# Softmax statistics of a quantised cross-attention: row maxima taken from logits in PSUM, row sums by a product with ones

## The chip, the cores and the metric

The kernel runs on one core of a Trainium2 chip. The core has five engines that each work through their own queue in order: TensorE (PE in the profile, with its weight loads shown apart as PEld), VectorE (DVE), ScalarE (ACT), GpSimd (POOL) and SyncE (SP), which here issues the transfers between HBM and SBUF. TensorE writes to PSUM, which is divided into eight banks of 128 partitions by 512 fp32 numbers[...]. Engines wait for each other by semaphores. The metric is the time of one execution on the device in microseconds (us), the median over several executions.

## The reference

Four transformer blocks follow one another, each with its own weights, on hidden states `x` of shape 4 x 1024 x 288 (batch, tokens, width), with a context of 4 x 64 x 288 that all of them attend to. Blocks 0 and 3 are attention, cross-attention and feed-forward with quantised linear layers; block 1 is a cross-attention; block 2, the one that matters here, quantises the operands of its attention. What is computed in its second attention, the cross-attention to the context, is this, with 16 heads of width 18 and 8 bits throughout:

```python
def _fake_quant(x, n_bits, always_zero=False):
    levels = float(2 ** n_bits - 1)
    if always_zero:
        delta = max(x) / levels; zp = 0.0
    else:
        delta = (max(x) - min(x)) / levels; zp = round(-min(x) / delta)
    xq = clip(round(x / delta) + zp, 0.0, levels)
    return (xq - zp) * delta

def _quant_attention(x, ctx, Wq, Wk, Wv, Wo, bo):
    q = x @ Wq; k = ctx @ Wk; v = ctx @ Wv           # split in 16 heads
    q, k, v = fake_quant of each
    probs = softmax(q . k / sqrt(18))                # 4 x 16 x 1024 x 64
    probs = _fake_quant(probs, 8, always_zero=True)
    return (probs @ v) @ Wo + bo

n2 = _ln(h, ln2_g, ln2_b)
h = h + _quant_attention(n2, encoder_hidden_states, Wq2, Wk2, Wv2, Wo2, bo2)
n3 = _ln(h, ln3_g, ln3_b)
a, gate = split(n3 @ Wff1 + bff1)
h = h + a * gelu(gate) @ Wff2 + bff2
```

The point to keep in mind is the step of the last quantisation, `delta`. It needs the largest probability over all batches, tokens, heads and context tokens, so no probability can be rounded before every one has been seen.

## The kernel before, in words

The 4096 tokens are handled as 32 tiles of 128 (`NT`, eight for each batch, `NTB`). Each head's 18 columns are padded to 32 (`HP`), so that four heads make a head group of 128 rows and there are four groups (`NG`). The blocks run one after the other, with some work of the next block placed in the current one: during block 2 the weights of block 3 are loaded (line L1568), and their quantisation scales are formed on DVE (lines L1581 to L1612, tiles called `ssw` and `wps`).

The function that the change touches is `fq_tail`. It does the context attention and the feed-forward of block 2. The queries before quantisation, `rawq`, lie in DRAM, with their global maximum and minimum known. Keys and values have been quantised and laid out as block-diagonal operands: `kbd4` holds, for each batch and head group, a 128 x 256 matrix whose four diagonal blocks are the keys of four heads, and `kbd` holds the same keys in the other orientation, in blocks of 64 rows for two heads. Because of `delta`, the attention makes two passes over the logits.

The *first pass* finds, for each token and head, the largest exponential (`top`, 128 x 32 x 16) and the sum of the exponentials (`sums`, of the same shape). Its loop takes the tiles one by one. For a tile t it does the following.

- DVE scales, shifts and rounds the queries in two operations (`fq_levels`, L818 and L819), and clips them in a third (L3302), which writes them as bf16 in the padded layout into one of three buffers, `pads`.
- TensorE transposes the four head groups (L3308) into a PSUM bank, ACT copies them to SBUF (L3312, `qT`), and SP stores them to DRAM (L3313, `qb`) for the second pass.
- TensorE makes the logits, tokens on partitions, in four bf16 products of 128 x 256 (L3318), two to a bank. ACT takes the exponential of each bank, 128 x 512 (L3325), into an SBUF tile `e` of 128 x 16 x 64 fp32. The softmax scale and the quantisation steps come in as the scale of this activation.
- DVE reduces `e` to its 16 maxima (L3331). GpSimd adds the two halves of every head's 64 exponentials (L3333, 512 outputs for each partition) and again the halves of these (L3335, 256 outputs), and DVE sums the 16 values that remain for each head (L3336).

No exponential of the first pass is shifted by a maximum. The PSUM pool of this stage, `psum8`, has eight buffers of one bank; the SBUF pool of work tiles, `f2k0`, has three buffers for each kind of tile. The order in which the instructions of different tiles stand in each engine's queue is not that of the source: it is decided when the program is built, by the scheduler of the framework. An engine then follows its queue strictly.

After the loop `prob_shift` forms, on DVE, the reciprocals of `sums` (L2483), the product with `top`, the largest probability (across partitions with GpSimd), and a logarithmic shift for each token and head, split into three bf16 numbers (`parts`). The *second pass* (`probs`) begins with loads of `qT` from DRAM (L3362), adds the shift to spare rows of the queries, recomputes the exponentials in the transposed layout (context tokens on partitions), rounds them and multiplies them with the values. It is woven with the feed-forward (`forward`) of earlier tiles, and with block 3's weights. Ahead of it SP loads the feed-forward's weights (`w1` and `w2`, L2517, L114, L3352).

Two helpers return PSUM buffers: `ps1` a bank (from pool `pb`) and `ps2` two neighbouring banks (from pool `pa`). The pool set `psum_attn` exists already for other stages: three buffers of two banks and two of one bank.

Of the kernel before, what the change touches and what calls it, by code (L numbers as in the profile page):

```python
# [28 lines left out]
F32 = mybir.dt.float32  # L29
BF16 = mybir.dt.bfloat16  # L30
I32 = mybir.dt.int32
AF = mybir.ActivationFunctionType
ALU = mybir.AluOpType
AX = mybir.AxisListType
PSUM = bass.MemoryType.PSUM

P = 128
B, S, C, H, D, T, FF = 4, 1024, 288, 16, 18, 64, 1152
NTB = S // P
NT = B * NTB  # L40
CK, NC3 = 96, 3
HP = 32
NG = 4
# [1136 lines left out]
class Fast(Net):  # L1180
# [2080 lines left out]
    def fq_tail(self, w, kq, keep, rawq, mx, nmn, beside):  # L3261
# [4 lines left out]
        tc, nc = self.tc, self.nc  # L3266
        with ExitStack() as es:
# [4 lines left out]
            kt = {k: gp.tile(keep[k][1], BF16, name=k) for k in ("kbd", "vbd")}  # L3272
            qb = [dr.tile([P, NG, S], BF16, name=f"qb{b}") for b in range(B)]
            with (
                self.psum8("f2"),
                tc.tile_pool(name="f2q", bufs=1) as qp,
                self.work("f2k0", 3),
            ):
                kt["kbd4"] = qp.tile(keep["kbd4"][1], BF16, name="kbd4")
                for k, (d, _) in keep.items():  # L3280
                    nc.sync.dma_start(kt[k], d)
                top = qp.tile([P, NT, H], F32, name="top")
                sums = qp.tile([P, NT, H], F32, name="sums")
                qn = qp.tile([P, NT, C], F32, name="qn")
                for b in range(B):
                    nc.sync.dma_start(qn[:, b * NTB : (b + 1) * NTB, :], rawq[b])
                pads = [qp.tile([P, H, HP], BF16, name=f"pads{n}") for n in range(3)]
                for pd in pads:
                    nc.gpsimd.memset(pd, 0.0)
                q = self.global_params(gp, mx, nmn, "qq")  # L3290
                self.watch_range(-0.5, 255.5, q["zp"], "qzext")
                step = gp.tile([P, 1], F32, name="step")
                nc.vector.tensor_scalar(
                    step, q["d"], kq["d"][:, 0:1], SCALE, ALU.mult, ALU.mult
                )
                rstep = self.scale_register("cstep", step)

                for t in range(NT):
                    b, j = divmod(t, NTB)
                    pd = pads[t % 3]  # L3300
                    self.fq_levels(qn[:, t, :], q, 0)
                    nc.vector.tensor_scalar(  # L3302
                        pd[:, :, :D], self.heads(qn[:, t, :]), q["top"], None, ALU.min
                    )
                    ps = self.ps1(BF16)
                    pf = pd.rearrange("p h d -> p (h d)")
                    for g in range(NG):
                        nc.tensor.transpose(  # L3308
                            ps[:, g * P : (g + 1) * P], pf[:, g * P : (g + 1) * P], self.idb
                        )  # L3310
                    qT = self.wk.tile([P, NG, P], BF16, tag="qT1", name="qT1")
                    nc.scalar.copy(qT, ps[:, : NG * P].rearrange("p (g t) -> p g t", t=P))  # L3312
                    nc.sync.dma_start(qb[b][:, :, j * P : (j + 1) * P], qT)  # L3313
                    e = self.wk.tile([P, H, T], F32, tag="e1", name="e1")
                    for m in range(2):
                        ps = self.ps1()
                        for g in (2 * m, 2 * m + 1):
                            nc.tensor.matmul(  # L3318
                                ps[:, (g % 2) * 256 : (g % 2 + 1) * 256],
                                lhsT=qT[:, g, :],  # L3320
                                rhs=kt["kbd4"][:, b, g, :],
                                start=True,
                                stop=True,
                            )
                        nc.scalar.activation(  # L3325
                            e[:, 8 * m : 8 * m + 8, :],
                            ps.rearrange("p (h k) -> p h k", k=T),
                            AF.Exp,
                            scale=rstep,
                        )  # L3330
                    nc.vector.tensor_reduce(top[:, t, :], e, AX.X, ALU.max)  # L3331
                    e2 = self.wk.tile([P, H, T // 2], F32, tag="e2", name="e2")
                    nc.gpsimd.tensor_tensor(e2, e[:, :, : T // 2], e[:, :, T // 2 :], ALU.add)  # L3333
                    e4 = self.wk.tile([P, H, T // 4], F32, tag="e4", name="e4")
                    nc.gpsimd.tensor_tensor(e4, e2[:, :, : T // 4], e2[:, :, T // 4 :], ALU.add)  # L3335
                    nc.vector.tensor_reduce(sums[:, t, :], e4, AX.X, ALU.add)  # L3336
                pd, parts = self.prob_shift(gp, qp, top, sums, step)
            pv = gp.tile([P, 1], F32, name="pv")
            nc.vector.tensor_tensor(pv, pd, kq["d"][:, 1:2], ALU.mult)
# [304 lines left out]
```

## Time and profile before

| What | Value |
|---|---|
| Time, median of 3 executions | 4930.05 us (4927.19 to 4931.08) |
| Profiled execution, its own time | 4923.53 us |
| Its span on the core | 4921.8 us, 63638 instructions |
| Mean granted TensorE clock | 0.852 |
| Busy: PE | 4244.9 us (86%), 23227 instructions |
| Busy: PEld | 1704.0 us (35%) |
| Busy: DVE | 3001.9 us (61%), 6707 instructions |
| Busy: ACT | 3066.1 us (62%), 4347 instructions |
| Busy: POOL | 1259.5 us (26%), 1900 instructions |

The span runs from the first to the last recorded instruction; the time of the execution holds a little more around it. In the views, a line such as L3331 is a line of the kernel's source, and `out<-in` names the tiles that an instruction writes and reads with their shape (partitions x elements). A group's line gives the number of its instructions, their busy time and the mean of one, and after that the time that the engine stood idle just before them with what ended most of that wait. In the view of the slices the span is cut into 40 equal parts; each digit is the busy share of one part in tenths, and the row PEclk gives the TensorE clock that was granted, in tenths of full speed. Busy time is an average over stages that have different limits, so that the shares in the table say little of any one stage; the stretch of the changed loop has to be read by itself.

### The profile page before, as it was taken

What the parts mean: (1) busy time and instruction counts of PE and PEld (TensorE: products, weight loads), DVE (VectorE), ACT (ScalarE), POOL (GpSimd) and SP (SyncE); (2) the same over time, 40 slices, a digit from 0 to 9 for tenths busy, and PEclk for the clock granted to TensorE, in tenths of its full rate; (3) what the DMA queues carried; (4) which work ended last, traced back from release to release, by engine and by line L of the source; (5) the groups of instructions that cost most, each with busy time, mean ns of one, the idle gap of its engine ahead of it and who ended that gap; (6) DMA issues with size and microseconds to landing.
All of it is one profiled execution on the core that took longest, in us unless ns stands there. A gap on an engine that the chain in (4) does not pass through costs nothing. (4 is left out here: it accounts for less than half of the span.)

```text
span 4921.8 us, 63638 instructions
## 1 busy us (share of the span) xinstructions
PE 4244.9 (86%) x23227; PEld 1704.0 (35%) x23227; DVE 3001.9 (61%) x6707; ACT 3066.1 (62%) x4347; POOL 1259.5 (26%) x1900
## 2 busy tenths in 40 slices
PE   4999998778998979998888873899998999998776
PEld 2223223445565411110233331455443223222343
DVE  8355445764654589999788878333235355445775
ACT  2776775665663279998888853212113776775796
POOL 2001001543222576410112224111111001003664
PEclk9999999889999955555688885899998999998888
DMA  3000002100001221000010022101000000001000
GB/s 84 3 5 21 10 10 75 41 31 7 11 15 52 114 63 33 26 7 0 22 28 24 23 93 69 32 10 34 1 3 17 2 4 29 7 12 38 12 17 21
DMA packets 137700, 135.98 MB, mean 28 GB/s; under 512 B 69276, under 2 KB 114972, under 8 KB 135712
## 3 DMA queue, kind: packets, MB, share of 16 engines
q1 hardware_dynamic: 136176, 128.13, 8.7%
q0 software_dynamic: 1200, 3.69, 0.3%
q8 instruction: 184, 3.01, 0.3%
q14 instruction: 140, 1.15, 0.1%
HBM read 79.92 MB, written 43.47 MB: 25 GB/s over the span
## 5 line engine op out<-in xcount | busy, mean ns | idle before, releaser
L2082 ACT ACTIVATE e<-ps 128x1024 f32<-128x1024 f32 x1024 | 992.6, 1021 | 412.5 <-PE ps L2072 405.2
L2072 PE MATMUL ps<-qT,kT 32*128 32x512 f32 x4096 | 625.9, 649 | 1.6 <-DVE sext L1994 1.6
L3110 DVE TENSOR_REDUCE top<-e 128x2 f32<-128x2048 f32 x256 | 563.5, 2274 | 13.9 <-ACT e L3103 13.8
L2028 PE MATMUL ps<-e,v 128*32 128x512 f32 x4096 | 556.8, 615 | 8.5 <-DVE oT L2039 8.5
L3479 PE MATMUL ps<-qk 32*128 32x512 bf16 x1024 | 499.7, 605 | 40.6 <-ACT e L3103 38.7
L3528 ACT ACTIVATE e<-ps 128x1024 f32<-128x1024 f32 x512 | 484.0, 1054 | 77.5 <-PE ps L3519 58.8
L3103 ACT ACTIVATE e<-ps 128x1024 f32<-128x1024 f32 x512 | 520.1, 1151 | 6.9 <-PE ps L3479 3.7
L1807 POOL TENSOR_TENSOR x<-x,y 128x288 f32<-128x288 f32 x192 | 153.3, 807 | 789.3 <-DVE y L1806 483.8
L3531 DVE TENSOR_SCALAR eb<-e 128x2048 bf16<-128x2048 f32 x256 | 321.8, 1261 | 47.2 <-ACT e L3528 45.0
L3519 PE MATMUL ps<-qk,kz 64*128 64x512 bf16 x1024 | 228.6, 444 | 43.5 <-ACT e L3528 40.3
L2546 PE MATMUL psf<-hT,w 128*128 128x512 f32 x576 | 257.9, 600 | 0.6 <-ACT hT L2538 0.6
L2072 PEld LDWEIGHTS ps<-qT,kT 32*128 32x128 f32 x4096 | 184.5, 185 | 201.9 <-issue 128.7
L1427 POOL TENSOR_TENSOR h<-h,g 128x288 f32<-128x288 f32 x160 | 130.7, 818 | 427.4 <-ACT h L1424 417.9
L2028 PEld LDWEIGHTS ps<-e,v 128*32 128x32 f32 x4096 | 81.7, 109 | 403.9 <-issue 345.2
L3479 PEld LDWEIGHTS <-qk 32*128 32x128 bf16 x1024 | 53.2, 100 | 464.7 <-issue 463.7
L3428 ACT ACTIVATE gl<-psf,bf 128x512 f32<-128x512 f32 x72 | 46.0, 684 | 269.2 <-PE psf L2550 264.7
L1924 POOL TENSOR_TENSOR v<-y,wv1b 128x288 f32<-128x288 f32 x64 | 51.7, 812 | 563.3 <-DVE y L1921 563.3
L1356 ACT COPY qT<-ps 128x640 bf16<-128x640 bf16 (+3 forms) x252 | 149.4, 640 | 74.4 <-PE ps L1351 74.2
L1351 PE MATMUL ps<-idb,q 128*128 128x128 bf16 (+2 forms) x1128 | 108.2, 241 | 89.8 <-ACT q L1335 58.9
L3432 DVE SCALAR_TENSOR_TENSOR u<-psf,bf,gl 128x512 f32<-128x512 f32 x72 | 51.1, 746 | 218.5 <-ACT gl L3428 218.5
L278 PEld LDWEIGHTS <-qT 98*128 98x128 bf16 (+2 forms) x1344 | 133.8, 104 | 119.6 <-issue 47.0
L2039 DVE COPY oT<-ps 128x512 f32<-128x512 f32 x64 | 44.1, 690 | 211.3 <-PE ps L2028 211.3
(509 smaller groups left out, 7877.2 us busy)
## 6 DMA issues: line engine op xcount, KB each, us to landing
raw<-y SPq DMA_DIRECT2D x32, 432.0 KB
in<-raw SPq DMA_DIRECT2D x30, 432.0 KB
kz<-qk SPq DMA_DIRECT2D x128, 64.0 KB
wn<-in_L_wfc SPq DMA_DIRECT2D x12, 432.0 KB
x<-in_x SPq DMA_DIRECT2D x4, 1152.0 KB
vvo<-vt SPq DMA_DIRECT2D x16, 288.0 KB
vo<-vvo SPq DMA_DIRECT2D x4, 1152.0 KB
rawq<-y SPq DMA_DIRECT2D x32, 144.0 KB
```

Source lines behind the costliest of these rows:

```text
L1356: nc.scalar.copy(qT[:, c0 : c0 + r, j0 * P : (j0 + per) * P].rearrange("p c (a t) -> p a c t", a=per), ps[:width, : per * r * P].rearrange ...
L1807: nc.gpsimd.tensor_tensor(self.x[:, t, :], self.x[:, t, :], y, ALU.add)
L2028: nc.tensor.matmul(acc[i * HP : (i + 1) * HP, :], lhsT=st["v"][:, kt, h * (D + 1) : h * (D + 1) + HP], rhs=es_[i // 2][:, i % 2, :], start ...
L2072: nc.tensor.matmul(pss[i // 2][:, i % 2, :], lhsT=self.row_tile(kT, i)[:, kt * P : (kt + 1) * P], rhs=self.row_tile(qT, i)[:, qh * 512 : ( ...
L2082: nc.scalar.activation(e, ps, AF.Exp, scale=SCALE)
L2546: nc.tensor.matmul(o, lhsT=lhs(i)[:, c, :], rhs=rhs(i)[:, c, :], start=(c == 0), stop=False)
L3103: nc.scalar.activation(e[:, j, :].rearrange("p (a n) -> p a n", a=2), sc, AF.Exp, scale=rstep, accum_out=sums[:, t, h0 + j : h0 + j + 1],)
L3110: nc.vector.tensor_reduce(top[:, t, h0 : h0 + 2], e, AX.X, ALU.max)
L3479: self.last = self.nc.tensor.matmul(ps[:, c, :], lhsT=self.row_tile(qT, i)[:, g, qt * P : (qt + 1) * P], rhs=self.row_tile(kT, i)[:, g, c ...
L3519: nc.tensor.matmul(pss[i][:, n, :], lhsT=kz[rows, i, kt * P : (kt + 1) * P], rhs=qT[rows, g, qh * 512 : (qh + 1) * 512], start=True, stop= ...
L3528: nc.scalar.activation(e[:, 2 * n : 2 * n + 2, :], ps, AF.Exp, scale=step)
L3531: nc.vector.tensor_scalar(eb, e, MAGIC, MAGIC, ALU.add, ALU.subtract)
```

## The change

The first pass of block 2's context attention is rewritten. The stage's PSUM becomes `psum_attn`. Two constants are made by GpSimd ahead of the loop: `pick`, 128 x 2 x 32 in fp32, whose column k is one on the 64 rows that belong to head k of a group, and `back`, 128 x 16, a selection of columns of the identity.

`largest(t, qT)` is the part for one tile. Quantisation, transposes, copy and store are as before, but the copy goes to a quarter of a `qT` tile that holds four tiles' tokens. The four products of logits go to one buffer of two banks, and DVE reduces the logits to their maxima straight from PSUM. The exponential is applied to the finished `top` once, at the end of the loop.

`total(n, qT)` is the part for the sums of four tiles, 512 tokens. For each head group TensorE makes the logits a second time, with context tokens on the partitions (two products of 64 x 512), ACT takes their exponential (128 x 1024, fp32), and two fp32 products with `pick` add the exponentials over the partitions, into 32 partitions of an accumulator bank `acc` for each group. ACT copies the accumulator to SBUF (`sT`), four small fp32 products with `back` turn it so that tokens lie on partitions, and DVE copies the 128 x 64 result into `sums`. `total` is a generator with a pause after each exponential and after the copy; the loop advances it by one step after each tile of the next four. GpSimd's two additions and DVE's sum are gone.

```diff
@@ -3272,7 +3272,7 @@
             kt = {k: gp.tile(keep[k][1], BF16, name=k) for k in ("kbd", "vbd")}
             qb = [dr.tile([P, NG, S], BF16, name=f"qb{b}") for b in range(B)]
             with (
-                self.psum8("f2"),
+                self.psum_attn("f2"),
                 tc.tile_pool(name="f2q", bufs=1) as qp,
                 self.work("f2k0", 3),
             ):
@@ -3295,7 +3295,19 @@
                 )
                 rstep = self.scale_register("cstep", step)
 
-                for t in range(NT):
+                pick = qp.tile([P, 2, HP], F32, name="pick")
+                nc.gpsimd.memset(pick, 0.0)
+                for k in range(4):
+                    rows = slice(k % 2 * 64, (k % 2 + 1) * 64)
+                    nc.gpsimd.memset(pick[rows, k // 2, k : k + 1], 1.0)
+                back = qp.tile([P, H], F32, name="back")
+                nc.gpsimd.tensor_copy(
+                    back.rearrange("p (g i) -> p g i", i=4),
+                    self.idf.rearrange("p (g k) -> p g k", k=HP)[:, :, :4],
+                )
+
+                def largest(t, qT):
+
                     b, j = divmod(t, NTB)
                     pd = pads[t % 3]
                     self.fq_levels(qn[:, t, :], q, 0)
@@ -3308,32 +3320,64 @@
                         nc.tensor.transpose(
                             ps[:, g * P : (g + 1) * P], pf[:, g * P : (g + 1) * P], self.idb
                         )
-                    qT = self.wk.tile([P, NG, P], BF16, tag="qT1", name="qT1")
                     nc.scalar.copy(qT, ps[:, : NG * P].rearrange("p (g t) -> p g t", t=P))
                     nc.sync.dma_start(qb[b][:, :, j * P : (j + 1) * P], qT)
-                    e = self.wk.tile([P, H, T], F32, tag="e1", name="e1")
-                    for m in range(2):
-                        ps = self.ps1()
-                        for g in (2 * m, 2 * m + 1):
+                    ps = self.ps2()
+                    for g in range(NG):
+                        nc.tensor.matmul(
+                            ps[:, g // 2, g % 2 * 256 : (g % 2 + 1) * 256],
+                            lhsT=qT[:, g, :],
+                            rhs=kt["kbd4"][:, b, g, :],
+                            start=True,
+                            stop=True,
+                        )
+                    nc.vector.tensor_reduce(
+                        top[:, t, :], ps.rearrange("p a (h k) -> p (a h) k", k=T), AX.X, ALU.max
+                    )
+
+                def total(n, qT):
+
+                    acc = self.ps1()
+                    for g in range(NG):
+                        ps = self.ps2()
+                        for pr in range(2):
+                            rows = slice(pr * 64, (pr + 1) * 64)
                             nc.tensor.matmul(
-                                ps[:, (g % 2) * 256 : (g % 2 + 1) * 256],
-                                lhsT=qT[:, g, :],
-                                rhs=kt["kbd4"][:, b, g, :],
-                                start=True,
-                                stop=True,
+                                ps[:, pr, :], lhsT=kt["kbd"][rows, n // 2, g, :],
+                                rhs=qT[rows, g, :], start=True, stop=True,
                             )
-                        nc.scalar.activation(
-                            e[:, 8 * m : 8 * m + 8, :],
-                            ps.rearrange("p (h k) -> p h k", k=T),
-                            AF.Exp,
-                            scale=rstep,
+                        e = self.wk.tile([P, 2, 512], F32, tag="e1", name="e1")
+                        nc.scalar.activation(e, ps, AF.Exp, scale=rstep)
+                        yield
+                        for pr in range(2):
+                            nc.tensor.matmul(
+                                acc[g * HP : (g + 1) * HP, :], lhsT=pick[:, pr, :],
+                                rhs=e[:, pr, :], start=(pr == 0), stop=(pr == 1),
+                            )
+                    sT = self.wk.tile([P, 512], F32, tag="sT", name="sT")
+                    nc.scalar.copy(sT, acc)
+                    yield
+                    ps = self.ps1()
+                    for j in range(4):
+                        nc.tensor.matmul(
+                            ps[:, j * H : (j + 1) * H], lhsT=sT[:, j * P : (j + 1) * P],
+                            rhs=back, start=True, stop=True,
                         )
-                    nc.vector.tensor_reduce(top[:, t, :], e, AX.X, ALU.max)
-                    e2 = self.wk.tile([P, H, T // 2], F32, tag="e2", name="e2")
-                    nc.gpsimd.tensor_tensor(e2, e[:, :, : T // 2], e[:, :, T // 2 :], ALU.add)
-                    e4 = self.wk.tile([P, H, T // 4], F32, tag="e4", name="e4")
-                    nc.gpsimd.tensor_tensor(e4, e2[:, :, : T // 4], e2[:, :, T // 4 :], ALU.add)
-                    nc.vector.tensor_reduce(sums[:, t, :], e4, AX.X, ALU.add)
+                    nc.vector.tensor_copy(
+                        sums[:, 4 * n : 4 * n + 4, :].rearrange("p t h -> p (t h)"),
+                        ps[:, : 4 * H],
+                    )
+
+                running = []
+                for n in range(NT // 4):
+                    qT = self.wk.tile([P, NG, 512], BF16, tag="qT1", name="qT1")
+                    for j in range(4):
+                        largest(4 * n + j, qT[:, :, j * P : (j + 1) * P])
+                        running = [t for t in running if next(t, running) is not running]
+                    running.append(total(n, qT))
+                while running:
+                    running = [t for t in running if next(t, running) is not running]
+                nc.scalar.activation(top, top, AF.Exp, scale=rstep)
                 pd, parts = self.prob_shift(gp, qp, top, sums, step)
             pv = gp.tile([P, 1], F32, name="pv")
             nc.vector.tensor_tensor(pv, pd, kq["d"][:, 1:2], ALU.mult)
```

## The prediction

> **What bounds the kernel now.** I read the page's slices first, to find the stage, and the granted TensorE clock beside it.
>
> ```profile
> PE   4999998778998979998888873899998999998776
> DVE  8355445764654589999788878333235355445775
> PEclk9999999889999955555688885899998999998888
> ```
>
> A slice is 123 us. The changed loop lies in slice 24 (2952 to 3075), the only one in the middle where PE falls to 3, and the clock there is 5, half. Stretches of the trace around it (columns: PE, PEld, DVE, ACT, POOL busy, clock, DMA share, GB/s):
>
> ```profile
> core 0: us, PE busy (x) PEld busy (x) DVE busy (x) ACT busy (x) POOL busy (x), PEclk, DMA share, GB/s
> 1750.00:2300.00 550.00, 506.00 (x1216) 73.02 (x1217) 536.11 (x253) 524.68 (x1012) 239.87 (x265) 0.50 0.08 23
> 2940.00:3044.00 104.00, 49.65 (x256) 27.51 (x256) 93.86 (x168) 53.03 (x97) 64.27 (x64) 0.50 0.26 66
> 3128.00:3188.00 60.00, 60.00 (x204) 32.73 (x203) 16.74 (x55) 6.89 (x11) 4.54 (x6) 1.00 0.01 1
> ```
>
> The loop takes 104 us; DVE is busy in 93.9 of them, TensorE in 49.7. Note the row above it: PE busy in 92% of the time does not bring the full clock. The groups of the stage (out<-in, count | busy us, mean ns | idle before, releaser):
>
> ```profile
> L3333 POOL TENSOR_TENSOR e<-e 128x512 f32<-128x512 f32 x32 | 40.5, 1265 | 38.9 <-ACT e L3325 38.5
> L3331 DVE TENSOR_REDUCE top<-e 128x16 f32<-128x1024 f32 x32 | 38.6, 1208 | 3.1 <-ACT e L3325 3.0
> ...
> L3308 PE MATMUL ps<-idb,pads 128*128 128x128 bf16 x128 | 19.9, 311 | 33.3 <-DVE pads L3302 33.3
> L819 DVE TENSOR_SCALAR qn<-qn,qqnzp 128x288 f32<-128x288 f32 x32 | 19.1, 598 | 0.0
> ...
> L818 DVE TENSOR_SCALAR qn<-qn,qqrd 128x288 f32<-128x288 f32 x32 | 15.5, 494 | 0.0
> L3302 DVE TENSOR_SCALAR pads<-qn,qqtop 128x288 bf16<-128x288 f32 x32 | 14.2, 443 | 0.0
> ...
> L3336 DVE TENSOR_REDUCE sums<-e 128x16 f32<-128x256 f32 x32 | 13.0, 407 | 7.1 <-POOL e L3335 7.1
> ```
>
> So DVE bounds the loop: TensorE's largest wait, 33.3 us, is for DVE's padded queries. The loop's last sum (L3336) ends at 3044.06, and the chain to the second pass starts there:
>
> ```profile
> 3043.64 0.42 DVE L3336 TENSOR_REDUCE sums<-e 128x16 f32<-128x256 f32 x1 [0.36 <-POOL e L3335]
> 3043.98 0.16 DVE L1584 TENSOR_SCALAR ssw<-ssw 128x4 f32<-128x4 f32 x1
> 3044.05 0.15 DVE L1583 TENSOR_TENSOR ssw<-wps 128x4 f32<-128x4 f32 x1
> 3044.12 3.35 DVE L2483 RECIPROCAL rs<-sums 128x512 f32<-128x512 f32 x1
> ```
>
> Every microsecond by which the last sum moves, the end moves.
>
> [...] L819 has a median of 362 ns but a mean of 598 and a longest of 1312. [...] The trace agrees on the window (its clock changes at multiples of 3.41 us). To find the measure I weighted each product's streaming time by its share of array rows times columns, window by window over the whole trace: a window at half clock is followed by full clock from a share of 0.72 up (7 of 378 windows contradict), a full one is followed by half below 0.37 (9 of 915). Busy time alone separates worse (23 contradict). [...] the trace shows some 0.15 us (eight 128*32 products of 0.43 us of streaming hold TensorE for 0.58 at 3118.16).
>
> **The change part by part.** *Removed:* GpSimd's halvings (40.5 + 24.0 us), DVE's 32 sum reductions (0.33 us from start to start, 10.5), and the blocking: L818, L819 and L3302 cost 48.8 us where 32 x 3 x 0.28 = 27 would do. DVE would need 0.84 + 1.2 = about 2.05 us a tile (the maximum now comes from PSUM[...]) and a 64-element copy per four tiles: some 66 us, plus about 14 of block 3's weights (some 6 of them now in the stage, the rest behind it). The 64 exponentials of 128x512 become 32 of 128x1024 (such rows cost 1.02 to 1.05). All this buys nothing unless DVE still bounds.
>
> *Added on TensorE:* 64 bf16 products of 64x512 (in pairs on two row tiles, 0.43 us a pair at half clock) and 64 fp32 products of 128x512 with 32 output columns. What fp32 costs is in other stages:
>
> ```profile
> 834.89 2.07 PE L2311 MATMUL ps<-qcT,kbd 64*128 64x512 f32 x2
> ...
> 3769.27 1.94 PE L2028 MATMUL ps<-e,v 128*32 128x512 f32 x8
> ```
>
> The first is one fp32 product at half clock: two passes. The second is four, side by side on four column tiles, again two passes; the trace's starts lie 0.855 us apart. In the changed kernel the two products of a head group accumulate in the same 32 partitions, so they stand behind one another: 4 passes, 3.42 us. At full clock a pass is 0.43.
>
> *The order.* In the changed program TensorE's queue holds, for each tile from the fifth on: four logit products, one pair of transposed logit products of the previous four tiles, four transposes of the next tile, then the two fp32 products, which wait for the exponential of that pair. Behind them in the queue stands the next tile's work, and DVE and ACT wait for that. A round at half clock: logits 0.85, tiling change 0.15, pair 0.43, to ACT 0.2, exponential 1.03, back 0.06 (these two steps as between L3318, L3325 and the next), fp32 3.42, tiling change 0.15: 6.29 us. The transposes (0.43) hide in the exponential's wait; without that cover they would add 0.43. DVE's 2.05 and ACT's 1.6 hide in the round.
>
> The sum: the first four tiles without fp32 work, until the fifth's padded queries come through DVE behind four maxima, 9.6; 28 rounds, 176.0; seven group ends, where the ACT copy, four fp32 turning products (8 passes of 0.21, as for other short fp32 products at half clock) and the DVE copy stand ahead of the fp32 pair, 1.7 each, 11.9; the tail: 3.7 to the first product, 13 passes of 0.854 (neighbours lie on different column tiles, so the last pass of one can overlap the first of the next), 11.1, copy, turning and DVE copy 3.2. Together 215.5, from 2940.5: last sum at 3156.0 against 3044.06, +111.9.
>
> *Given back:* block 3's weight operations (L1584 to L1612), which stand between the links of the chain after 3044, move ahead into DVE's slack: -2.5. The added exponential of the maxima (128x512, about 0.6) comes before the last sum: nothing; were it late it would cost 0.6. Of DMAs, the 32 stores of qT stay, one a tile, and the loads behind the chain keep their order; the two small stores of block 3's scales (L1793) move ahead between them on SP's queue, and would hold up the stores behind them if the weights were late, which matters only when a qT buffer is needed again, three groups or some 75 us later. GpSimd's new constants (pick, back) are set before 2938, where it is idle for 10.8 us. *Unknown:* the start could reach the full clock for a window or two (two transposes, two logit sets, two transposes without a gap give over 0.8): -2, between 0 and -15. [...] Group ends 0.8 to 2.5 each: -6 to +6. Tail 15 to 22: -3 to +4.
>
> **Does the clock stay at half?** The round's array share at half clock is (0.85 + 0.43 + 0.43 + 0.25 x 3.42) / 6.29 = 0.41; its densest 3.41 us hold 0.59, under 0.72. If it is full at first, a round is 3.7 us and its share 0.34, under 0.37, and it falls back. So half.
>
> Result: +111.9 - 2.5 - 2 = +107.4. On the profiled execution: span 4921.8 + 107.4 = 5029.2, and with the 1.7 around it (4923.53 - 4921.8) 5030.9. The timed runs' median, 4930.05, is 6.5 above the profiled 4923.53; with the same distance, 5037.
>
> **Rivals.** *Full clock* (0.08): 9.6, 28 rounds of 3.7, seven ends of 0.9 and a tail of 10 make 129.5 against 103.6, and with the 2.5 given back +23, 4953. For it: 0.34 is near 0.37, and the trace has a few full windows under 0.37 that stayed full. Against: it would have to hold some 35 windows in a row, and nothing in a round at half clock lifts it again. *Longer rounds* (0.04): the exponential or the logits also wait for PSUM, since the pool has three two-bank buffers and two single ones, one of them held over four rounds by the accumulator: 7.2 a round, 25 more, 5062. For it: before, all eight banks were single buffers; against: in a round of 6.3 us each reader (DVE 1.2, ACT 1.03) has long been done. *DVE's relief decides* (0.03), the faster case: place, TensorE's queue; point, a round below (106 - 9.6 - 6 - 9) / 28 = 2.9 us; then the loop shrinks toward DVE's 81 us, -23 - 2.5, 4905. For it: DVE's 93.9 of 104 us, and GpSimd's blocking of it, are real. Against: at full clock the round without fp32 work is 2.0, so that its four passes would have to take 0.23 us each; no row shows one under 0.43. It is also the case in which the products with ones vanish in the wait for ACT, which their place in the queue, behind that wait, forbids. *No net change* (0.02): the same with a round of 2.9 to 3.1.
>
> **How the numbers follow.** Forecast 0.83; the unknowns' ends, not all at once, give its own range, 5006 to 5058. Full clock, no change and faster, 0.13 together, stay outside below; longer rounds begin above 5050. Range, widened to meet these and a clock that is full for a few windows more: 5002 to 5062. Faster by over 0.2% (about 10 us, what a measurement here can tell from no change): 0.03; within: 0.02; slower: 0.95.
>
> **What would show it.** The fp32 rows busy for some 109 us with 128 passes, pitch 0.85; clock 0.50 in the stage; TensorE idle about 0.9 us a round before the fp32 pair, for ACT; L818, L819 and their follower near 360 ns; no GpSimd work; last copy of sums near 3156. Wrong if the clock rises, if passes on one column tile overlap, or if the rounds are not serial.

## The result, and the profile after

The changed kernel took 4953.7 us in the median of five runs (4951.0 to 4957.77), the kernel before 4927.19 beside it (4924.1 to 4931.08). The ratio is 1.0057 with a 95% interval of 1.0045 to 1.0068: slower, by some 26 us. The forecast was 5037 us with a range of 5002 to 5062. The side was right and the size wrong by a factor of four: +107 us were expected. The time is that of the first rival, the one in which TensorE's clock is full, at 4953; that it fits to a microsecond is in part luck, since this rival added 23 us to 4930.05 and the kernel took 26.5 more than 4927.19.

The page's slices of the kernel after show where the forecast failed. A slice is 123.9 us; slice 24, counted from 0 as in the forecast, runs from 2973.6 to 3097.5 and holds most of the loop.

```profile
PE   4999998888998979997888867799998999998676
DVE  8355435755654689999788775333234355445775
PEclk9999998889999955555788889799998999998888
```

The granted clock in slice 24 is 9, where the kernel before had 5. The same in the stretches of the trace (columns as before: PE, PEld, DVE, ACT, POOL busy, clock, DMA share, GB/s). The first row is the loop, from its first transposes to its last sum; the next two are consecutive windows of 3.41 us near its beginning.

```profile
2945.30:3080.50 135.20, 109.30 (x512) 39.95 (x512) 78.01 (x170) 54.61 (x74) 0.00 (x0) 0.94 0.19 50
...
2959.89:2963.30 3.41, 3.41 (x12) 0.81 (x10) 1.50 (x2) 0.26 (x1) 0.00 (x0) 0.50 0.02 5
2963.30:2966.72 3.42, 2.84 (x13) 0.76 (x10) 2.17 (x8) 1.24 (x2) 0.00 (x0) 0.95 0.15 38
```

DVE, the busiest engine of the loop before (93.9 of 104 us), is busy in 78.0 of 135.2 us; TensorE now leads with 109.3. The clock becomes full at about 2963 and stays so until the loop ends. The groups of the stage, in the kernel after:

```profile
L3353 PE MATMUL ps<-e,pick 128*32 128x512 f32 x128 | 60.7, 613 | 20.0 <-ACT e L3350 17.9 <-DVE sums L3366 2.0
L3334 DVE TENSOR_REDUCE top<-ps 128x16 f32<-128x1024 f32 x32 | 39.0, 1224 | 43.1 <-PE ps L3327 42.9
...
L3320 PE MATMUL ps<-idb,pads 128*128 128x128 bf16 x128 | 14.2, 241 | 12.6 <-DVE pads L3314 12.6
...
L819 DVE TENSOR_SCALAR qn<-qn,qqnzp 128x288 f32<-128x288 f32 x32 | 11.3, 365 | 0.0
```

The wait has changed sides, as forecast: DVE stands idle 42.9 us for the logits, where before TensorE waited 33.3 us for DVE. The fp32 products with ones are the largest group, and TensorE waits 17.9 us ahead of them for the exponential. One round of TensorE's queue, at full clock (start, duration, idle time before in brackets):

```profile
2980.36 1.90 PE L3353 MATMUL ps<-e,pick 128*32 128x512 f32 x4 [0.85 <-ACT e L3350]
2982.20 0.61 PE L3327 MATMUL ps<-kbd,qT 128*128 128x256 bf16 x4
2982.74 0.39 PE L3345 MATMUL ps<-qT,kbd 64*128 64x512 bf16 x2
2983.06 0.40 PE L3320 MATMUL ps<-idb,pads 128*128 128x128 bf16 x4
2984.31 0.62 PE L3353 MATMUL ps<-e,pick 128*32 128x512 f32 x1 [0.85 <-ACT e L3350]
```

From one fp32 group to the next it is 3.95 us. This is the order of work that the forecast had, step for step, at twice the speed.

One caution on comparing two traces. The loop's first transposes stand at 2940.47 in the trace before and at 2945.33 in the trace after, and in the other traces of this study anywhere from 2940.4 to 2952.4, since the stages ahead of the loop, which nobody changed, vary. So the length of the loop is compared below and not the instant at which it ends: 103.6 us before (to 3044.06), 135.2 after (to 3080.48), +31.6. After the last sum, 1877.7 us remained before (4921.8 - 3044.06) and 1875.5 after (4956.0 - 3080.48), 2.2 fewer. That makes +29.4, against +26.5 between the medians.

### The profile page after: what moved, and what is told of

Its sections match the earlier page's. It is cut to its first block, busy times and chain, and to the rows that moved or that the text cites. A ratio compares the mean times of both kernels' runs of the same rounds, so it can differ in the third digit from the quotient of the medians.

```text
span 4956.0 us, 63976 instructions
## 1 busy us (share of the span) xinstructions
PE 4311.1 (87%) x23483; PEld 1719.2 (35%) x23483; DVE 2980.0 (60%) x6683; ACT 3068.1 (62%) x4324; POOL 1195.8 (24%) x1842
## 5 line engine op out<-in xcount | busy, mean ns | idle before, releaser
L1351 PE MATMUL ps<-idb,q 128*128 128x128 bf16 (+2 forms) x1128 | 109.6, 243 | 90.2 <-ACT q L1335 58.9
L3103 ACT ACTIVATION_READ_ACCUMULATOR e<-ps 128x1 f32 x512 | 172.3, 337 | 0.0
```

Of the source, the lines that this page charges most:

```text
L3103: nc.scalar.activation(e[:, j, :].rearrange("p (a n) -> p a n", a=2), sc, AF.Exp, scale=rstep, accum_out=sums[:, t, h0 + j : h0 + j + 1],)
```

## The experiments

### What the clock follows

The forecast took from the trace of before that the clock follows the share of array rows times columns. The products with ones use 32 of 128 columns, so they counted for a quarter. Counting again with rows alone (the time in which each product streams, times its rows out of 128, summed over a window of 3.41 us; products that run at once count together for at most the whole array) gives for the window that ends at 2963.3 a share of 0.81 (0.43 with columns), and for the full windows of the loop 0.52 to 0.78 (0.24 to 0.40 with columns). With bounds like the forecast's, 0.72 or 0.73 to rise and 0.37 to stay, rows times columns contradict the trace after in 33 of 946 full windows, 28 of these in this loop; rows alone contradict it in 3, none in the loop. To test this on the chip I left the number of products and their columns as they were, and cut the number of rows that the products with ones read. In these three runs the ones stand on all rows, so the sums are not the reference's; the runs differ from each other in the number of rows alone.

```diff
-    for k in range(4):
-        rows = slice(k % 2 * 64, (k % 2 + 1) * 64)
-        nc.gpsimd.memset(pick[rows, k // 2, k : k + 1], 1.0)
+    nc.gpsimd.memset(pick[:, :, 0:4], 1.0)
...
-    acc[g * HP : (g + 1) * HP, :], lhsT=pick[:, pr, :],
-    rhs=e[:, pr, :], start=(pr == 0), stop=(pr == 1),
+    acc[g * HP : (g + 1) * HP, :], lhsT=pick[:32, pr, :],
+    rhs=e[:32, pr, :], start=(pr == 0), stop=(pr == 1),
```

With 32 rows:

> The changed kernel with the fp32 products of ones reading only 32 of the 128 partitions of the exponentials (so the sums miss three quarters of their terms; the maxima and all other work are as in the changed kernel). Instructions, passes and streaming time are the same. If the clock is granted by the share of array rows in use, whatever the columns: a round at half clock holds (0.85 + 0.43 + 0.43 + 0.25 x 3.42) / 6.29 = 0.41 and its densest window about 0.53, under 0.73, and a round at full clock 0.32, under 0.37: the clock stays at 0.5, the round is about 6.3 us, the time about 5030. If any busy time of TensorE counts: clock full and round 3.95 us as in the changed kernel, about 4954.

Measured: 5035.62 us against 4922.83 before, ratio 1.023 (1.0211 to 1.0249). With 64 rows:

> The same with 64 of the 128 partitions (the sums miss half of their terms). By rows: a round at half clock holds 0.55, its densest window about 0.68, just under 0.73, so the clock is more likely to stay at half, 5030; a full window or two would lift it, and then 0.43 a round is enough to keep it full, 4955. If any busy time counts: 4954.

Measured: 5028.96 against 4922.83, ratio 1.0216 (1.0198 to 1.0235). With 96 rows:

> The changed kernel with the products of ones reading 96 of the 128 partitions of the exponentials (the sums miss a quarter of their terms). By rows in use with a bound of 0.73 in one window: a round at half clock has its densest window at (0.75 x 2.1 + 1.28) / 3.41 = 0.84, over the bound, so the clock rises as in the changed kernel and stays (a round at full clock holds 0.54): about 4954. If something else than the number of rows made the runs with 32 and 64 partitions slow, such as products of less than the whole height, it stays at half: about 5030.

Measured: 4959.23 against 4922.78, ratio 1.0074 (1.0045 to 1.0103). The group of the products with ones, in the traces with 32, 64 and 96 rows:

```profile
L3351 PE MATMUL ps<-e,pick 32*32 32x512 f32 x128 | 109.6, 1055 | 16.8 <-ACT e L3348 14.8 <-DVE sums L3364 2.0
```

```profile
L3351 PE MATMUL ps<-e,pick 64*32 64x512 f32 x128 | 109.6, 1056 | 16.8 <-ACT e L3348 14.8 <-DVE sums L3364 2.0
```

```profile
L3351 PE MATMUL ps<-e,pick 96*32 96x512 f32 x128 | 60.7, 613 | 20.2 <-ACT e L3348 18.2 <-DVE sums L3364 2.0
```

The same 128 passes take 109.6 us with up to 64 rows and 60.7 with 96 or 128. Stretches inside the loop show the clock with it, for 64 rows first and then for 96:

```profile
2960.00:3050.00 90.00, 82.80 (x218) 24.16 (x217) 39.62 (x89) 21.26 (x29) 0.00 (x0) 0.50 0.08 21
```

```profile
2960.00:3050.00 90.00, 73.48 (x349) 26.08 (x348) 56.91 (x130) 35.93 (x49) 0.00 (x0) 0.99 0.13 33
```

With 64 rows TensorE is busy in 92% of the time and stays at half; with 96 it is busy in 82% and runs at full clock. Since a full clock itself makes TensorE less busy, two single windows at half clock say it better, one with 64 rows and the one with 96 rows after which the clock rose:

```profile
2998.64:3002.05 3.41, 3.41 (x5) 0.48 (x4) 0.65 (x3) 0.18 (x2) 0.00 (x0) 0.50 0.15 38
```

```profile
2957.77:2961.18 3.41, 3.41 (x9) 0.72 (x9) 1.50 (x2) 0.00 (x0) 0.00 (x0) 0.50 0.11 29
```

Both are busy from end to end. So busy time does not decide it. By rows, the highest share in the loop, ahead of its tail, that did not lift the clock was 0.57 with 32 rows and 0.69 with 64, while 0.74 (96 rows) and 0.81 (128) lifted it. All three results, and the changed kernel, follow from rows alone with a bound near 0.73. That the columns do not count is shown by the changed kernel itself, where 32 columns were enough.

The tail of the run with 64 rows tells how rows have to be counted. There the products of three head groups run side by side, on three column tiles and the same 64 rows (twelve passes in the window below, where in the run with 32 rows four on one column tile take 3.62 us):

```profile
3138.58:3142.00 3.42, 3.31 (x12) 0.40 (x6) 0.00 (x0) 0.03 (x1) 0.00 (x0) 0.50 0.00 0
```

If their rows are added, this window holds 0.91, and the clock should have risen; it stayed at half. Counted once, the rows make 0.45. So in this window rows that several column tiles share count once.

One rival remains after these runs, since the window that lifted the clock with 96 rows would also have done so if a product of more than 64 rows counted as one of the whole height (0.87 in place of 0.74). The trace of before speaks against it, for it has many products of 96 and 98 rows: counting these as 128 takes the windows that contradict from about a dozen to over thirty. The clock of these traces changes at multiples of 3.41 us, and what went ahead of the rise in the loops with 96 and 128 rows was a window with 0.74 and 0.81 of the rows in use, where one with TensorE just as busy and 64 rows did not lift it.

The runs with 32 and 64 rows are also the forecast carried out at the clock that it assumed. This is TensorE's queue in the trace with 32 rows:

```profile
2999.20 3.62 PE L3351 MATMUL ps<-e,pick 32*32 32x512 f32 x4 [0.64 <-ACT e L3348]
3002.75 1.03 PE L3325 MATMUL ps<-kbd,qT 128*128 128x256 bf16 x4
3003.72 0.61 PE L3343 MATMUL ps<-qT,kbd 64*128 64x512 bf16 x2
3004.26 0.60 PE L3318 MATMUL ps<-idb,pads 128*128 128x128 bf16 x4
3005.51 3.62 PE L3351 MATMUL ps<-e,pick 32*32 32x512 f32 x4 [0.65 <-ACT e L3348]
```

The round is 6.31 us where the sum had 6.29, the loop 208.8 us with 32 rows and 209.1 with 64 where it had 215.5, the time 5036 and 5029 where it had 5037.

### What the added pass costs

Here the second set of exponentials and everything after it is left out.

```diff
-    running = []
+    nc.vector.memset(sums, 64.0)
     for n in range(NT // 4):
         qT = self.wk.tile([P, NG, 512], BF16, tag="qT1", name="qT1")
         for j in range(4):
             largest(4 * n + j, qT[:, :, j * P : (j + 1) * P])
-            running = [t for t in running if next(t, running) is not running]
-        running.append(total(n, qT))
-    while running:
-        running = [t for t in running if next(t, running) is not running]
```

> The changed kernel without the second, transposed set of exponentials and its products: the sums are set to a constant, so the output is not the reference's. It prices the added pass. If TensorE's queue of the added products bounds the changed loop, the loop falls to DVE's 2.05 us a tile and some of block 3's weights, 2.2 x 32 + 9 = about 80 us, with the clock at half (1.28 / 2.2 = 0.58 of rows): about 60 us less than the changed kernel, 4893. If DVE's quantising and maxima bounded it, less than 20 us.

Measured: 4899.6 against 4922.83, ratio 0.9956 (0.9941 to 0.9971). The loop lasts 77.2 us from its first transposes to its last maximum. The added pass thus costs 1.0057 - 0.9956 = 1.0%, some 50 us of the changed kernel; of these about 3 belong to the reciprocal of the sums (L2483, 3.35 us), which with a constant runs ahead of the loop. Without the sums, the quantising and the maxima alone are 23 us faster than the kernel before, the same 3 us included. The change had some 20 us to spend, and spent more than twice as much on TensorE.

### Where the 50 us lie: the passes and the wait

First the passes. Exponentials and ones in bf16, all else as in the changed kernel:

```diff
-    pick = qp.tile([P, 2, HP], F32, name="pick")
+    pick = qp.tile([P, 2, HP], BF16, name="pick")
...
-    e = self.wk.tile([P, 2, 512], F32, tag="e1", name="e1")
+    e = self.wk.tile([P, 2, 512], BF16, tag="e1", name="e1")
```

> The changed kernel with the exponentials of the second set and the ones in bf16, so that each product is one pass and not two at half the rate. By rows, a round at half clock of some 3.7 us holds 0.69, denser windows over 0.73: the clock becomes full. A round at full clock loses 1.84 - 0.43 = 1.4 us of products; then the chain through ACT (pair 0.32, exponential 1.1, copy of the queries 0.6, logits 0.54, hand-overs) sets about 2.7 us: 28 x 1.25 = 35 us less, about 4919. If the clock falls back to half: a round of 3.7 to 3.9, about 4950. If fp32 were not the price: 4954.

Measured: 4920.15 against 4922.83, ratio 0.9996 (0.9988 to 1.0005). That is 0.6% less than the changed kernel: fp32 is the larger part of the price. The trace has a loop of 99.8 us, rounds of 2.64 us once the clock is full, but this comes only at 2981, after six rounds of some 3.7 us. Fewer passes also mean fewer rows in use: by the starts in the trace a round of 3.64 us at half clock has 2.56 us of streaming on all rows, a share of 0.70, just under the bound; the fp32 round at half clock, with the forecast's terms, has 5.13 of 6.29 us, 0.82. That the clock rose later for this is my estimate.

Then the wait. In the source, a tile's transposes and copy come after the products with ones of the step before. Writing them one tile ahead changes the order in the queue (fp32 as in the changed kernel):

```diff
+    ready(0, quarter(0))
     for n in range(NT // 4):
-        qT = self.wk.tile([P, NG, 512], BF16, tag="qT1", name="qT1")
+        qT = qTs[n]
         for j in range(4):
-            largest(4 * n + j, qT[:, :, j * P : (j + 1) * P])
+            if 4 * n + j + 1 < NT:
+                ready(4 * n + j + 1, quarter(4 * n + j + 1))
+            largest(4 * n + j, quarter(4 * n + j))
```

`ready` is the first half of `largest`, down to the store of qT; `largest` keeps the logits and the maxima; `quarter(t)` gives tile t's quarter of its `qT` tile.

> The changed kernel, fp32 as it is, with only the order changed: quantising, transposes and copy of the next tile ahead of the logits of this one (PSUM as in the changed kernel). If the wait of 0.85 us a round for the exponential is real idle time on the path, a round goes from 3.95 to about 3.2 (1.84 + 0.54 + 0.32 + 0.4): 28 x 0.75 = 20 us less, about 4933. If the fp32 passes alone set the round, 4954.

Measured: 4936.28 against 4923.29, ratio 1.0028 (1.0017 to 1.0038), about 14 us less than the changed kernel. The wait ahead of the products with ones all but goes:

```profile
L3357 PE MATMUL ps<-e,pick 128*32 128x512 f32 x128 | 59.0, 607 | 4.4 <-ACT e L3354 3.3 <-DVE sums L3370 0.3
```

20.0 us of waiting become 4.4, the round 3.40 us in place of 3.95 (3.2 was expected), and the loop 115.7. So the 0.85 us a round was on the path, and with it gone the kernel with its fp32 passes is still slower than before.

Both together, with the stage's PSUM as two buffers of two banks and four of one bank, so that the transposes do not wait for the bank that holds the accumulator:

> The bf16 version, with quantising, transposes and copy of the next tile written ahead of the logits of this one, and the stage's PSUM as two two-bank and four one-bank buffers: in the queue the products of ones then come behind the next logits and no longer behind the exponential just started. At full clock TensorE then needs 0.54 + 0.53 + 0.32 + 0.4 = 1.8 us a tile, ACT 1.7, DVE 2.05 and block 3's weights: if the waits for ACT were what is left of the round of 2.64, DVE bounds and the round is about 2.3, and less idle time lifts the clock sooner (0.9 of rows at half clock): some 20 to 25 us less than the bf16 version, about 4898. If the PSUM buffers or the hand-overs set the round, 4920 as there.

Measured: 4905.52 against 4923.29, ratio 0.9963 (0.9949 to 0.9976): 0.4% faster than the kernel before, and 0.9% faster than the changed one. The loop lasts 84.1 us, from 2952.35 to 3036.48, and the groups show DVE almost without waits:

```profile
L3347 DVE TENSOR_REDUCE top<-ps 128x16 f32<-128x1024 f32 x32 | 38.9, 1216 | 2.1 <-PE ps L3340 2.0
...
L3366 PE MATMUL ps<-e,pick 128*32 128x512 bf16 x64 | 19.6, 388 | 2.6 <-ACT e L3363 1.7
```

This is the version in which the idea of the change pays, with sums of exponentials that are rounded to bf16: DVE hardly waits any more, with a smaller load than before. Its last maximum ends 75.7 us after the first transposes, as early as in the kernel without any sums (77.2). What the sums still cost in the loop is the tail, the 8.4 us from there to the last sum, in which the last group's exponentials, products and copies follow one another with no tile's work beside them. How much of the gain belongs to the PSUM buffers alone was not tested.

### What bounded the loop before

The forecast read DVE as the bound before: busy, and slowed in a part of its work by GpSimd. One part of the change alone tests it: the maxima from PSUM, with exponentials, halvings and sums as before.

```diff
-    self.psum8("f2"),
+    self.psum_attn("f2"),
...
-        for m in range(2):
-            ps = self.ps1()
+        pss = self.ps2()
+        for m in range(2):
+            ps = pss[:, m, :]
...
-        nc.vector.tensor_reduce(top[:, t, :], e, AX.X, ALU.max)
+        nc.vector.tensor_reduce(
+            top[:, t, :], pss.rearrange("p a (h k) -> p (a h) k", k=T), AX.X, ALU.max)
...
+    nc.scalar.activation(top, top, AF.Exp, scale=rstep)
```

> The kernel before with one part of the change alone: the logits of a tile in one two-bank PSUM buffer, the maxima reduced from there, and the exponential of the maxima at the end; exponentials, GpSimd's halvings and DVE's sums as before. If DVE's busy time and its blocking by GpSimd bound the loop of before, nothing is gained but the 3 us that DVE waited for the exponential ahead of the maximum: 4920 to 4927. If the wait for the exponential were the bound, some 10 us less.

Measured: 4927.02 against 4923.29, ratio 1.0007 (0.9998 to 1.0016): no difference. Inside, however, much has moved. Groups of the stage:

```profile
L3336 POOL TENSOR_TENSOR e<-e 128x512 f32<-128x512 f32 x32 | 40.1, 1258 | 43.4 <-ACT e L3326 34.6 <-ACT qT L3312 8.7
...
L3339 DVE TENSOR_REDUCE sums<-e 128x16 f32<-128x256 f32 x32 | 13.4, 419 | 20.1 <-POOL e L3338 20.1
...
L819 DVE TENSOR_SCALAR qn<-qn,qqnzp 128x288 f32<-128x288 f32 x32 | 11.6, 363 | 0.0
L818 DVE TENSOR_SCALAR qn<-qn,qqrd 128x288 f32<-128x288 f32 x32 | 11.6, 363 | 0.0
```

The stretch of 104 us that the forecast showed, in the same columns (PE, PEld, DVE, ACT, POOL busy, clock, DMA share, GB/s):

```profile
2940.00:3044.00 104.00, 50.96 (x256) 25.34 (x256) 80.62 (x166) 53.62 (x96) 60.45 (x63) 0.52 0.26 65
```

GpSimd works as long as before, and yet L819 has fallen from a mean of 598 ns to 363. In exchange DVE waits 20.1 us for the halvings, where it had waited 7.1. The order of DVE's queue is another: quantising comes in bursts of several tiles while GpSimd is idle. DVE's busy time in 104 us falls from 93.9 to 80.6, and the loop goes from 103.6 to 105.8. The time is the one that was expected if DVE's busy time and its blocking were the bound, but not for that reason: 13 us of busy time went, and the loop did not get shorter. So DVE's busy time as such was not the bound. Does DVE's place in the chain behind GpSimd hold it? I took the last reduction away as well, and kept the maxima from PSUM and the halvings.

```diff
+    nc.vector.memset(sums, 64.0)
...
-    nc.vector.tensor_reduce(sums[:, t, :], e4, AX.X, ALU.add)
```

> The kernel before with the maxima taken from PSUM (the run called max only), and in addition without DVE's last reduction of the sums, which become a constant (so the sums are left out of the output); GpSimd's two additions stay and take as long. In the run with the maxima alone DVE lost 13 us of busy time in the stage and gained 12 us of waits for GpSimd, and the loop stayed at some 105 us. If it is DVE's place in the chain, waiting in its queue for the halvings, that holds that loop, it falls without the reduction to about 80 to 85 us, near the run without sums (77 us): about 4903. If GpSimd's own work or its access to SBUF holds it, it stays over 95 us: about 4918 or more.

Measured: 4911.2 against 4922.06, ratio 0.9973 (0.9961 to 0.9984), between the two expectations (about 3 us of the gain is again the reciprocal, which runs ahead of the loop). The loop lasts 88.6 us to its last maximum, and the blocking is back:

```profile
L818 DVE TENSOR_SCALAR qn<-qn,qqrd 128x288 f32<-128x288 f32 x32 | 17.5, 561 | 0.0
L819 DVE TENSOR_SCALAR qn<-qn,qqnzp 128x288 f32<-128x288 f32 x32 | 16.1, 513 | 0.0
```

Either DVE waits for the halvings in its queue or it runs beside them and is slowed by them: the two took each other's place in three kernels with the same GpSimd work: L818, L819 and the clip cost 48.8 us before, 35.5 with the maxima alone and 49.2 here, and the waits for GpSimd were 7.1, 20.1 and none. The slowing can be read in the trace of before: of the 96 operations on these three lines, the 59 that ran while GpSimd was idle took 351 to 367 ns each, and all 27 that took more than 400, up to 1312, ran beside one of its additions (ten more met an addition and took 351 to 393). The run with the maxima alone shows that taking away the slowing gained nothing while the wait remained. The run here takes 13 us of DVE's own work away together with the wait, so it does not tell what the wait alone was worth. Of the rest, the loop of 88.6 us against the 77.2 without sums, I did not separate GpSimd's slowing from ACT's 64 exponentials; that stays open.

## Why the prediction was wrong, point by point

**The clock: wrong, and the whole of the error.** The step that failed is "so half", in the paragraph on whether the clock stays at half. Its measure, a product's share of array rows times columns, gave the round 0.41 and its densest window 0.59. By rows alone the changed kernel's second window with fp32 work held 0.81, and the clock rose in the second round of such products; the two runs in which it stayed at half, with 32 and 64 rows, took 5036 and 5029 us, close to the forecast. In 96% of the windows of the trace before, both measures differ by less than 0.05, since there products of few columns mostly run side by side on several column tiles (the first four passes of 32 columns at 3769.27 us start within 0.02 us), and their shares add up to the whole. A single product of 32 columns, repeated on one tile, was new, and the forecast carried the measure to it without asking whether other measures fitted the old trace as well. They did: rows alone contradict that trace in 5 of 378 half and 6 of 915 full windows, rows times columns, by the forecast's own count, in 7 and 9. The evidence was even in the trace: of the 17 windows in which the two part by more than 0.1, three decide between them, and all three for rows (at 895 us a share of 0.78 by rows and 0.65 with columns, and at 4503 us 0.85 and 0.45, rose to full clock; at 4824 us 0.42 and 0.28 stayed full). The first rival said that the clock would have to hold 35 windows with nothing to lift it; it held for 34, at a row share of 0.52 to 0.78.

**The rounds: right in mechanism and size, given the clock.** At half clock 6.31 us against 6.29. For full clock the rival had 3.7, where the terms of the round at that clock (0.43 + 0.15 + 0.21 + 0.2 + 1.03 + 0.06 + 1.71 + 0.15) make 3.94; measured, 3.95. The rival's sum for the whole loop, 129.5 us, against 135.2: the first four tiles took 9.6 as forecast; the rounds are 28 x 0.25 = 7 longer; the two rounds before the clock rose cost 3.1 (4.60 and 6.38 against 3.95 each); a group's end cost 0.5 us and not 0.9 (four rounds take 16.31 us), 2.8 less; the tail 8.9 and not 10. Together 129.5 + 7 + 3.1 - 2.8 - 1.1 = 135.7.

**Two passes for an fp32 product, one behind the other on a column tile: right.** 128 passes for the 64 products of the source, 0.43 us apart at full clock; at half clock the next product follows the first of four passes after 3.55 us (2999.20 to 3002.75 in the lines above).

**The wait for ACT ahead of the products with ones: right.** 0.85 us a round at full clock, and the run with the order changed shows that it was on the path.

**PSUM buffers: right, as far as it goes.** In the changed kernel TensorE waits only 0.8 us behind DVE's maxima and 2.0 us behind its copies of the sums, so that longer rounds from the buffers did not come.

**DVE's relief: right that it would not decide, wrong in what it rested on.** L818, L819 and the clip fell to a mean of 365 ns, 33.8 us of busy time where before there were 48.8. But DVE's busy time as such was not what bounded the loop before, as the run with the maxima alone shows; slowing by GpSimd and waiting for GpSimd stood in for each other. The gain to be had was there all the same, 23 us. Reading the maxima from PSUM cost little: they took 1224 ns in place of 1208.

**Given back: right.** 2.2 us after the last sum, against 2.5.

**The chances.** The forecast gave 0.83 to one reading of the clock. With two measures that the trace at hand hardly told apart, the case of full clock deserved far more than 0.08, and the range should have reached it.

## What to carry to other kernels

Before a rule fitted to one trace is carried to a new kind of instruction, list the other rules that fit that trace about as well and see where they part for the new one; here the two parted by 80 us. In these runs, work for the TensorE clock is counted by rows in use: products over all 128 partitions with 32 columns kept the clock full at a row share of 0.52 and more, and the same products over 64 rows, with TensorE busy in 92% of the time, did not lift it. And when an engine is both slowed by a neighbour and waits for it, look at both together: here an order that parted the two in time gained nothing, since the wait took the place of the slowing (20.1 us in place of 7.1, with L819 at 363 ns in place of 598); taking the waiting step away gained 11 us, with the slowing back; leaving out the sums altogether, and with them the neighbour's work, gained 23.

## What the runs showed of the hardware that I had not expected

The same fp32 products ran at nearly twice the speed when they read 96 partitions in place of 64: 60.7 us in place of 109.6, and 70 us less for the kernel. In none of these runs did reading fewer rows make anything faster. In the other direction, the bf16 version, with 64 passes in place of 128 and a pair of products in 0.53 us at full clock where the fp32 pair takes 1.84, had its clock rise 18 us later than the fp32 version (2981 against 2963), which took back part of its gain.
